# A four-layer transformer whose queues are ordered by a planner: the order by a hand-written key replaced by one that lays the steps out forwards and backwards, with durations from the trace

## The chip, the cores and the metric

The kernel runs on one core of a Trainium2 chip. Its time is in device microseconds (us): the time of one execution on the device, and over several runs their median. The engines are named as in the profile: PE is TensorE's matmuls and PEld its loads of weights, DVE is VectorE, ACT is ScalarE, POOL is GpSimd, SP is SyncE (which here only issues DMA transfers).

## The reference, cut to what matters

An input `x` of 2048 tokens by 128 channels passes through four layers. Each adds an attention and then a feed-forward part to `x`, and each part reads `x` after a norm over the channels without weights.

```python
x = x + attention_0(norm(x))  # 16 heads of 64, all 2048 keys, biases on q, k, v, out
x = x + experts(norm(x))      # 8 experts, each token to its argmax, at most 256 tokens each
x = x + attention_1(norm(x))  # 16 heads of 64, causal
x = x + mix(norm(x))          # sigmoid(xr Wr) * (relu(xk Wk)^2 Wv), xr and xk mixed with the token before
x = x + attention_2(norm(x))  # metric attention, 16 heads of 8
x = x + ffn_2(norm(x))        # relu, weights rounded to -1, 0, 1
x = x + attention_3(norm(x))  # 16 heads of 64, region mask, a bias from gelu/sigmoid features
x = x + ffn_3(norm(x))        # exact gelu, weights sign(w) * mean|w| by row
```

Within the experts a token's place is the count of earlier tokens with the same expert, so each chunk of tokens needs the counts of the chunks before it. All data are float32.

## The kernel before, in words

**Tiling.** `x` stays in SBUF as 16 tiles of 128 tokens. The three big attentions go through 8 pairs of heads, and each pair through 8 groups of 256 queries. A group is worked in this way: `score` (line 505) lets PE multiply keys and queries into PSUM banks; `scan` (L515) has DVE copy a bank to SBUF and take its minimum (queries carry the opposite sign, so the minimum is the peak); `spread_lowest` gathers the minima over partitions (POOL L561, DVE L564, and L569 on POOL where the layer has a bias) and hands them out (L575, on ACT, in the causal layer on POOL); `exps` (L587) has ACT take the exponentials and their sums; `turn` has DVE transpose blocks of 32 by 32 (L614), and in the layers without a causal mask PE transposes the last 128 keys of the group's last quarter instead (L622), which ACT copies back (L625); `weigh` (L646) multiplies by the values; `sum_up` (L667 on PE, L687 and L690) gives the inverse sums; `project_out` multiplies by the output weights (L704 on PE), divides on ACT (L714), and adds to `x` on POOL (L732). Projections of keys and queries are L399, of values L420. The pairs overlap: the next pair's projections and scores run beside the weighing of the last group.

**Between the attentions.** Here the work goes by chunks of tokens as soon as the last pair has left them. `normalise` takes statistics on DVE (L250), raises to a power on POOL (L255 to L257), scales (L260 on ACT; L265 on another engine for some tiles), transposes on PE (L271), and copies on ACT (L286). `experts` takes logits on PE (L886), subtracts the peak (L890, DVE), takes the exponential (ACT), chooses on DVE (`choose`, L894 to L901), counts on PE (`count`, L905), forms weights on DVE (`weights`, L910 to L916), transposes them on PE (`turn`, L920), multiplies by the biases (L924) and the experts (L947). After layer 1 follow the mix (`rest`: L1119 and L1142, L1123, gate L1127), the product that stands for layer 2's attention (L1131; its weights collapse to one 128 by 128 matrix, made ahead in `folded`), the ternary feed-forward (`feed_forward`: L989, activation L998, L1014), another norm, and the features of layer 3 (L1229, gelu L1234, L1242, sigmoid L1259, L1248). Weights of the last feed-forward part are binarised by `binary` (DVE L1283 to L1291, transposed on PE, L1301) while layer 3's attention runs.

**Steps, rings and the planner.** No instruction is issued where it is written down. Each piece of work is a `Step` with an engine, a believed duration in us, the steps that it follows, the buffers that it takes or uses, and a key: a tick of a time-table written by hand (`planner(tick, place)`), a place within the tick, and a running number. Buffers come from a `Ring` of a fixed number of tiles. In most rings the order in which steps take buffers is fixed by their keys; in three (PSUM tiles `MISC`, the norms' `MEANS` and `NORMED`) it is open. A step that takes a buffer waits for all users of the one it replaces.

At the end `run` (L120) puts all steps into the five engines' queues. It simulates the queues with the believed durations, 0.15 us for a hand-over between engines (`HOP`) and 1.3 us where ACT must load another function table. Each time it looks on each engine through the open steps in order of their key, takes the first that can start at once, or one that would be done before a better one starts, and of the five engines' finds the one that starts earliest; that step is issued next on its engine. Every engine then works through its queue in order, waiting by semaphores.

```python
for s in [next_[e]] if next_[e] else sorted(open_[e], key=lambda s: s.key):
    t = None if s.left else s.ready()
    if t is None:
        continue
    t = max(t, free[e])
    if found is None or t + us(s) <= found[0] + 0.1:
        found = (t, s)
    if found[0] <= free[e]:
        break
```

## Time and profile before

| what | value |
|---|---|
| median of 3 runs | 3465.9 us (3461.34 to 3470.4) |
| profiled execution | 3463.54 us |
| its span, first to last instruction | 3461.8 us |
| mean granted clock of TensorE | 0.987 of full speed |
| busy time of PE, DVE, ACT, POOL | 3378.0, 3211.7, 2810.9, 951.3 us |
| layer 0's attention, one pair in steady state | 147.1 us |
| layer 1's, one pair in steady state | 96.4 us |
| layer 3's, one pair in steady state | 149.5 us |
| loads of function tables on ACT | 30, 1283 ns each |

The profile is of one execution on the core. Its busy times are sums over the instructions of an engine; PE and PEld overlap each other. The stages follow one another in this order: a start of 27 us, layer 0's attention to about 1140 us, the experts and the start of layer 1 to about 1380, layer 1's attention to about 1990, mix, layer 2 and the start of layer 3 to about 2260, layer 3's attention to about 3340, and the end. The granted clock is what the throttle allows TensorE, as a share of full speed; a window of the trace gives its mean in that window. In a line on waits, the first name is the instruction that waits, and the one behind the arrow is what ended the wait. In a line of the timeline the bracket at the end holds the idle time ahead of an instruction, and what released it.

### The profile page before, as it was taken

How to read it: one execution, taken by the hardware profiler on the slowest of the kernel's cores; microseconds unless marked ns; L12 is line 12 of the kernel's file. 1: busy time of each engine (PE TensorE's matmuls, PEld its weight loads, DVE VectorE, ACT ScalarE, POOL GpSimd, SP SyncE). 2: the span in 40 equal slices, each digit the busy share in tenths (PEclk: the TensorE clock that was granted, in tenths of full speed). 3: DMA queues.
4: the chain of work that ended last, by engine and by line, in shares of the span. 5: the costliest groups of instructions: out<-in, count | busy, mean ns of one | idle time of the engine just before them, and what ended most of it. 6: DMA issues, size and time to landing. Idle time of an engine off the chain costs nothing.

```text
span 3461.8 us, 115408 instructions
## 1 busy us (share of the span) xinstructions
PE 3378.0 (98%) x46922; PEld 1819.8 (53%) x46922; DVE 3211.7 (93%) x8019; ACT 2810.9 (81%) x8712; POOL 951.3 (27%) x2821
## 2 busy tenths in 40 slices
PE   8999999999999899999999998899999999999999
PEld 3545454554545455555555654455555555555555
DVE  7999999999999878999999885699999999999996
ACT  5888888888888767888888876688888878888886
POOL 2121222212222343223232354222222222222233
PEclk9999999999999999999999999899999999999999
DMA  1000000000000000000000000000000000000000
GB/s 48 2 5 2 5 5 2 5 2 5 2 5 5 2 5 8 6 6 6 6 6 3 7 5 4 4 5 5 2 5 2 5 5 2 5 2 2 2 5 11
DMA packets 22960, 18.98 MB, mean 5 GB/s; under 512 B 3556, under 2 KB 21612, under 8 KB 22426
## 3 DMA queue, kind: packets, MB, share of 16 engines
q1 hardware_dynamic: 22362, 11.55, 1.2%
q8 instruction: 367, 6.01, 0.7%
q14 instruction: 167, 1.37, 0.1%
q0 software_dynamic: 64, 0.06, 0.0%
HBM read 10.60 MB, written 1.05 MB: 3 GB/s over the span
## 4 chain that ended last, share of the span: by engine, by line
PE 82%; DVE 11%; ACT 4%; issue 2%; POOL 1%; DMA 0%; SPq 0%; POOLq 0%; DVEq 0%; ACTq 0%
PE s L505 33%; PE o L646 32%; DVE e L515 5%; PE pp L399 5%; DVE e L614 3%; PE y L704 3%; PE pv L420 3%; ACT e L587 2%; PE t L622 2%; PE ps L667 1%; PE pe L947 1%; PE ph L989 1%; PE po L1014 1%; PE pt L271 0%; DVE st L250 0%
## 5 line engine op out<-in xcount | busy, mean ns | idle before, releaser
L587 ACT ACTIVATE e<-e,shift 128x512 f32<-128x512 f32 (+14 forms) x3072 | 1973.7, 649 | 26.3 <-POOL shift L575 18.6
L515 DVE TENSOR_SCALAR_CACHE_REDUCE e<-s 128x512 f32<-128x512 f32 (+15 forms) x3072 | 1659.0, 589 | 95.8 <-PE s L505 94.2
L505 PE MATMUL s<-kT,qT 64*32 64x512 f32 (+8 forms) x24576 | 1463.3, 535 | 20.6 <-DVE e L515 20.5
L614 DVE STREAM_TRANSPOSE e<-e 128x2048 f32<-128x2048 f32 (+10 forms) x768 | 1435.4, 1871 | 15.0 <-ACT e L587 12.9
L646 PE MATMUL o<-e,v 128*64 128x256 f32 (+1 forms) x10496 | 1272.6, 374 | 2.6 <-DVE e L614 2.4
L646 PEld LDWEIGHTS o<-e,v 128*64 128x64 f32 x10496 | 747.1, 137 | 549.3 <-issue 300.9
L505 PEld LDWEIGHTS s<-kT,qT 64*32 64x32 f32 x24576 | 417.0, 105 | 518.2 <-issue 220.6
L587 ACT ACTIVATION_READ_ACCUMULATOR e<-e,shift 128x1 f32 x3072 | 591.9, 193 | 0.0
L561 POOL COPY low<-low 32x8 f32<-32x8 f32 x1152 | 208.9, 181 | 1236.9 <-DVE e L515 1200.1
L732 POOL TENSOR_TENSOR x<-x,part 128x256 f32<-128x256 f32 x384 | 280.9, 731 | 269.3 <-ACT part L714 253.8
L575 ACT COPY shift<-shift 32x8 f32<-32x8 f32 x768 | 150.0, 195 | 134.7 <-POOL shift L569 88.1
L714 ACT ACTIVATE part<-y,r 128x128 f32<-128x128 f32 x768 | 217.6, 366 | 38.7 <-PE y L704 36.9
L515 DVE DVE_READ_ACCUMULATOR e<-s 128x1 f32 x3072 | 231.0, 75 | 0.0
L687 POOL TENSOR_TENSOR r<-r,inverse 128x4 f32<-128x4 f32 x128 | 130.3, 1018 | 322.5 <-ACT r L690 322.2
L399 PE MATMUL pp<-xT,w 128*128 128x512 f32 x384 | 213.7, 646 | 0.7 <-ACT xT L286 0.7
L646 PE MATMUL o<-e,va 128*64 128x128 f32 x1024 | 196.2, 273 | 0.0
L719 ACT COPY oT<-o 128x256 f32<-128x256 f32 x192 | 70.5, 367 | 154.6 <-PE o L646 153.9
L505 PE MATMUL s<-beyond,eye 64*32 64x32 bf16 x2560 | 160.0, 177 | 0.0
L704 PE MATMUL y<-w,oT 64*128 64x128 f32 x1536 | 139.0, 297 | 0.9 <-DVE bias L1255 0.4
L704 PEld LDWEIGHTS y<-w,oT 64*128 64x128 f32 x1536 | 101.6, 186 | 67.1 <-issue 23.6
L505 PEld LDWEIGHTS <-regions 64*32 64x32 bf16 x1024 | 66.3, 93 | 117.3 <-issue 84.1
L646 PEld LDWEIGHTS o<-e,va 128*64 128x64 f32 x1024 | 126.6, 138 | 0.0
(190 smaller groups left out, 2051.2 us busy)
## 6 DMA issues: line engine op xcount, KB each, us to landing
w<-in_L_wq SPq DMA_DIRECT2D x24, 64.0 KB, 1.9
w<-in_L_wk SPq DMA_DIRECT2D x24, 64.0 KB, 2.1
w<-in_L_wv SPq DMA_DIRECT2D x24, 64.0 KB, 2.1
w<-in_L_wo SPq DMA_DIRECT2D x24, 64.0 KB, 2.0
x<-in_x SPq DMA_DIRECT2D x4, 256.0 KB, 4.7
out_x<-x SPq DMA_DIRECT2D x3, 256.0 KB, 2.3
wo<-in_L_wo SPq DMA_DIRECT2D x1, 512.0 KB
moe_w<-in_moe_w SPq DMA_DIRECT2D x1, 512.0 KB
```

The lines of the kernel that those rows point to most:

```text
L399: nc.tensor.matmul(pp.t, lhsT=self.w.t[:, which, :], rhs=xT[:, cols(4 * c, 4)], start=True, stop=True)
L505: nc.tensor.matmul(s[h].t[on, bass.ds(first, size)], lhsT=lhsT, rhs=rhs, start=m == 0, stop=m == len(terms) - 1,)
L515: nc.vector.tensor_scalar(self.e(h)[:, i, 0:n], s.t[:, 0:n], 1.0, None, ALU.mult, ALU.min, accum_out=self.lows[j].t[:, 0, 4 * h + i % 4 : ...
L561: nc.gpsimd.tensor_copy(low.t[0:Q, c], low.t[bass.ts(c, Q), 0])
L575: (nc.gpsimd.tensor_copy if causal else nc.scalar.copy)(shift.t[bass.ts(c, Q)], first())
L587: nc.scalar.activation(e, e, AF.Exp, bias=self.shifts[j].t[:, 4 * h + i % 4 : 4 * h + i % 4 + 1], scale=-1.0, accum_out=self.sums.t[:, h, ...
L614: nc.vector.transpose(rows()[:, :, 0:n], rows()[:, :, 0:n])
L646: nc.tensor.matmul(self.o.t[bass.ds(DH * h, DH), i0:i1, :], lhsT=lhsT, rhs=self.e(h)[:, i0:i1, bass.ts(t, Q)], start=t == 0, stop=t == las ...
L687: nc.gpsimd.tensor_tensor(some, some, inverse, ALU.pow)
L704: nc.tensor.matmul(y[h].t[:, bass.ts(j, P)], lhsT=oT.t[half, bass.ts(j, P)], rhs=pair.w.t[half, 3, :], start=True, stop=True,)
L714: nc.scalar.mul(part.t[:, j, :], y[h].t[:, bass.ts(j, P)], r.t[:, j, h : h + 1])
L732: POOL, 0.74, lambda part=part: nc.gpsimd.tensor_tensor(xs, xs, part.t, ALU.add), [divided], uses=[part]
```

## The change

Two things change. First, `run` no longer takes the plan that comes from the keys. The old loop becomes `forward(rank, last)`, which sorts the open steps by a given rank; only with `last` does it issue anything. `backward()` takes the plan of the last `forward` and lays every step out again from the end: each as late as the steps behind it allow, in a gap of its engine that still holds it. Behind a step stand those that use its result, the step glued to it, and those that take its buffer over in the plan. The latest start is the step's new rank. `run` makes a plan by key, then three times a backward and a forward pass, and issues the one of these three plans that ends first in the planner's own times. The order within the rings is by key as before.

Second, about 35 believed durations are set to those of the trace. No instruction of arithmetic or transfer is added or removed. The built program loads ACT's function tables 25 times and not 30, and has 754 semaphore instructions and not 709 on POOL (ACT 535 and not 539, DVE 415 and not 408, PE 154 and not 152).

```diff
-        for _ in range(len(steps)):
-            best = None
...
+        def forward(rank, last):
+
+            for ring in rings:
+                ring.held = []
+            for s in steps:
+                s.left, s.since, s.end = len(s.after) + len(s.order) + (s in glued), 0.0, None
...
+                    for s in [next_[e]] if next_[e] else sorted(open_[e], key=lambda s: rank[s]):
...
+                s.begun, s.end = start, start + us(s)
...
+                for h in s.takes:
+                    if last:
+                        h.t = h.ring.make(h.called)
+                    h.ring.held.append(h)
+                if last:
+                    s.do()
...
+        def backward():
+
+            later = {s: list(h for h, data in heirs[s] if data) for s in steps}
+            for s in steps:
+                if s.then:
+                    later[s].append(s.then)
+            for ring in rings:
+                for h, g in zip(ring.held, ring.held[ring.bufs :]):
+                    for u in h.users:
+                        later[u].append(g.by)
+            end = max(s.end for s in steps)
+            busy, latest = [[(end + 1.0, end + 1e6)] for _ in range(5)], {}
+            for s in sorted(steps, key=lambda s: (-s.end, -s.begun)):
+                t = end
+                for b in later[s]:
+                    if b is not s:
+                        t = min(t, latest[b] - (HOP if b.engine != s.engine else 0.0))
+                gaps, us = busy[s.engine], s.end - s.begun
+                k = 0
+                while True:
+                    low = gaps[k + 1][1] if k + 1 < len(gaps) else -1e6
+                    top = min(t, gaps[k][0])
+                    if top - us >= low - 1e-6:
                         break
+                    k += 1
+                latest[s] = top - us
+                gaps.insert(k + 1, (top - us, top))
+            return latest
+
+
+        forward({s: s.key for s in steps}, False)
+        found = []
+        for _ in range(3):
+            rank = backward()
+            if not forward(rank, False):
+                break
+            found.append((max(s.end for s in steps), len(found), rank))
+        forward(min(found)[2], True)
```

```diff
-        t = add(PE, 0.2 * n, turn, scales, takes=[pt], uses=[xn])
+        t = add(PE, 0.04 + 0.115 * n, turn, scales, takes=[pt], uses=[xn])
...
-            us = max(0.2, 0.06 + 0.00168 * n) + (0.1 if causal else 0.07 if masked else 0.0)
+            us = max(0.15, 0.02 + 0.00168 * n)
+            more = 0.29 if causal else 0.27 if masked else 0.13
...
-            turned = [add(DVE, 0.06 + 0.00436 * n, do, made, uses=self.rows)]
+            turned = [add(DVE, 0.05 + 0.00426 * n, do, made, uses=self.rows)]
...
-                add(PE, 0.75, turn_apart, made, takes=[pt], uses=self.rows)
-                turned.append(add(ACT, 0.6, copy, uses=[pt] + self.rows))
+                add(PE, 0.55, turn_apart, made, takes=[pt], uses=self.rows)
+                turned.append(add(ACT, 0.47, copy, uses=[pt] + self.rows))
...
-        made = add(DVE, 1.3, choose, [made], uses=[r])
+        made = add(DVE, 1.7, choose, [made], uses=[r])
         add(PE, 0.4, count, [made] + masks, takes=[pc], uses=[r])
-        made = add(DVE, 1.2, weights, routed[-1:], uses=[r, pc])
+        made = add(DVE, 1.65, weights, routed[-1:], uses=[r, pc])
...
-        add(PE, 0.8, biases, [made], takes=[pb], uses=[pickT])
+        add(PE, 1.35, biases, [made], takes=[pb], uses=[pickT])
...
-            read.append(add(PE, 1.25, make, [made], takes=pe + [parts], uses=[moe_w]))
+            read.append(add(PE, 1.92, make, [made], takes=pe + [parts], uses=[moe_w]))
...
-                s = add(DVE, 0.2 + 0.002 * n, magnitude, last, takes=[] if last else [low], uses=[w] + ([low] if last else []))
-                last = [add(DVE, 0.2 + 0.0035 * n, signed, [s], uses=[w, low])]
+                s = add(DVE, 0.38 + 0.00168 * n, magnitude, last, takes=[] if last else [low], uses=[w] + ([low] if last else []))
+                last = [add(DVE, 0.5 + 0.0032 * n, signed, [s], uses=[w, low])]
```

The other durations change in the same manner, most of them by 0.02 to 0.7 us, among them the value projection's copy, the sums' copy, the products and the features.

## The prediction

> **What bounds the kernel now.** I read the page's busy times first, then its chain that ended last.

> ```profile
> PE 3378.0 (98%) x46922; PEld 1819.8 (53%) x46922; DVE 3211.7 (93%) x8019; ACT 2810.9 (81%) x8712; POOL 951.3 (27%) x2821
> PE 82%; DVE 11%; ACT 4%; issue 2%; POOL 1%; DMA 0%; SPq 0%; POOLq 0%; DVEq 0%; ACTq 0%
> ```

> TensorE is busy for 3378.0 of 3461.8 us, so 83.8 us is all its idle time. The change alters no instruction of arithmetic; it can win back idle time, the time lost to a lowered clock, and time that ACT or DVE put on the chain. To see where those lie I cut the run into stages with the table of windows (columns: window in us, its length, busy time of PE, PEld, DVE, ACT and POOL with their counts, granted clock, DMA share, GB/s). These are the two joints between layers, one pair of heads in layer 3's steady state, and a later pair in which weights are binarised:

> ```profile
> 1140.00:1380.00 240.00, 221.77 (x2851) 119.82 (x2854) 203.52 (x665) 164.96 (x557) 95.76 (x230) 0.94 0.02 5
> 1990.00:2260.00 270.00, 236.41 (x2391) 131.56 (x2390) 188.36 (x579) 195.83 (x502) 102.97 (x234) 0.92 0.02 5
> 2506.00:2655.50 149.50, 149.50 (x2009) 79.25 (x2009) 146.83 (x305) 124.64 (x373) 38.14 (x120) 1.00 0.01 4
> 2803.80:2961.80 158.00, 155.63 (x2050) 81.91 (x2049) 156.02 (x325) 127.82 (x382) 38.60 (x122) 0.99 0.01 4
> ```

> The steady state has no idle TensorE at all. The joints idle for 240 - 221.8 = 18.2 and 270 - 236.4 = 33.6 us, and their clock of 0.94 and 0.92 costs another 0.06 x 240 = 14 and 0.08 x 270 = 22 us. Three quarters of the reachable time is here. TensorE's waits name its releasers (engine, line, releaser: us in total, times, longest):

> ```profile
> PE pt L271 <- ACT xn L260: 26.5, 8, 12.4
> PE s L505 <- DVE e L515: 20.5, 28, 2.8
> PE pick_turned L920 <- DVE routes L916: 6.4, 3, 2.8
> PE pc L905 <- DVE routes L901: 5.2, 4, 1.9
> ```

> The transposes of a norm (L271) wait for its scaling; 12.4 of their 26.5 us is the start of the program. The routing of layer 0's experts (L905, L920) waits for VectorE; the scores wait for scans to free their banks.

> **The change, part by part.** The built orders of the two kernels hold the same arithmetic on each engine. ACT loads a function table 25 times, not 30, and POOL has 754 semaphore instructions, not 709. POOL is 27% busy and SyncE's queue holds the same loads in almost the same order (a weight lands 2 us after its issue), so I price both at nothing; if a weight came late, it would cost those 2 us once.

> *Routing of the experts.* TensorE's timeline shows the wait in chunk 0, and what came after it:

> ```profile
> 1147.50 0.38 PE L905 MATMUL pc<-routes,earlier 128*128 128x32 f32 x2 [0.73 <-DVE routes L901]
> 1148.03 0.71 PE L704 MATMUL y<-w,oT 64*128 64x128 f32 x8
> 1151.53 1.01 PE L920 MATMUL pick_turned<-ident,routes 128*8 128x128 f32 x4 [2.79 <-DVE routes L916]
> 1153.21 2.07 PE L924 MATMUL pb<-moe_b,pickT 8*128 8x128 f32 x8 [0.66 <-ACT pickT L937]
> ```

> The planner believed 1.3 and 1.2 us for `choose` and `weights` and now believes 1.7 and 1.65, so it puts more TensorE work between them. By the new order, chunk 0 has four weighings and a query projection's part (0.8 us) ahead of L905: 0.73 goes, while the 2.79 stays. Chunk 1 has a projection and four weighings (1.0 + 1.05) between L905 and L920: its 2.79 becomes about 1.4 and its 0.72 nearly 0. Chunk 2 puts two projections ahead of L905, not one: 1.83 becomes 0.8. Chunk 3 puts 1.7 us ahead: 1.87 becomes 0.17, and 0.81 becomes 0.6. That is 0.73 + 1.39 + 0.65 + 1.03 + 1.70 + 0.21 = 5.7. What is taken from later work leaves a shorter queue there, so I take -4.5, bounds 0 and -5.7.

> *Clock.* After that stall the biases (L924) took 2.07 us; in chunk 2 the same row took 1.15. The windows 1153 to 1157 and 1213 to 1219 have a granted clock of 0.50 and 0.60, each after a stall of 2.79. A dip costs about 2 to 3 us (6 us at 0.60 loses 2.4). One of the two 2.79s shrinks, and the two of 1.8 go: I take one dip, -3. Bounds: 0, and -20 if about half of the 36 us of clock in both joints comes back. [...]

> *Layer 1 to layer 3.* The last four tiles pass norm, mix, product, FFN and norm one after another while little else is left:

> ```profile
> 2117.26 0.66 PE L271 MATMUL pt<-ident,xn 128*128 128x128 f32 x4 [1.86 <-ACT part L714]
> 2127.57 5.19 PE L646 MATMUL o<-e,v 128*64 128x256 f32 x48
> 2143.86 1.54 PE L271 MATMUL pt<-ident,xn 128*128 128x128 f32 x6 [6.74 <-ACT xn L260]
> ```

> In the new order the 48 weighings of 5.19 us and a product of 0.71 come ahead of the transposes at 2117.26. Of these 5.9 us, 1.86 falls in the stall there, so the norm may start 4.0 later; but the chain's later steps are then free of the 5.19. Between +4.0 and -1.2 I take +1, near the lower end, since TensorE idles 6.74 soon after. Moved out of the way: the mix of chunk 2 (L1142) no longer stands behind a weighing that took 0.61 + 3.50 and takes 1.95 at full clock elsewhere (-1.8, the part that is no stall and no longer slow); a first norm on POOL between another's powers and its scaling (-1.3, one such L255 to L257); a projection (L399, 1.13) now ahead of the features' weighing (-1). Before this, from 2010 to 2117, TensorE idles 107 - 97.6 = 9.4 us at clock 0.95; some steps there are reordered, none clearly for the better: -1. Together -4. Bounds: +5.9 with all of the weighing on the path, and -15 with the 9.4 and the 5.4 of its clock gone.

> *Function tables.* On ACT's timeline a load takes 1.28 us, and the exponential after it starts 1.30 after it:

> ```profile
> 2211.10 1.28 ACT L587 ACT_TABLE_LOAD   x1
> 2212.40 0.72 ACT L587 ACTIVATE e<-e,shift 128x512 f32<-128x512 f32 x1
> ```

> Three of the five saved loads are in layer 1's end, two in the last FFN, where ACT is on the chain: 2 x 1.28 = 2.6, and one of the three, 1.3, since the joint's waits are on ACT for half of their time: -3.9, bounds 0 and -6.4. [...]

> *Binarised weights.* Seven DVE pieces lay in one lump of 8.2 us (2798.6 to 2806.9), and TensorE ran dry behind the scans:

> ```profile
> 2804.00:2808.00 4.00, 1.78 (x16) 1.24 (x18) 3.86 (x9) 1.42 (x3) 0.00 (x0) 1.00 0.01 2
> 2808.00:2812.00 4.00, 4.00 (x40) 1.26 (x34) 4.00 (x9) 2.21 (x7) 0.39 (x2) 0.57 0.00 0
> ```

> The pair took 158.0 and the one ahead of it 148.4, against 149.5: 8.5 - 1.1 = 7.4 lost. The new order spreads the pieces one to a gap (DVE has 149.5 - 146.8 = 2.7 of slack in a pair) but for the last three, 0.93 + 1.25 + 2.1 = 4.3 in a row. With the loss in proportion, 7.4 x 4.3 / 8.2 = 3.9 stays: -3.5, bounds 0 and -5.5.

> *Start.* One more projection stands ahead of the first scores (1 us at a cold clock), and one less after them: +0.5, bounds -0.5 and +1.5.

> *Steady state.* Rings of buffers are still handed out by the hand-written key, so scans, weighings and scores keep their sequence, and DVE's order in a pair of layer 0 is identical. What moves is the transpose of a group's last quarter (L622), now ahead of about 5 us of TensorE work that it followed. I price it at 0 and cover it under the rivals.

> Sum: -4.5 - 3 - 4 - 3.9 - 3.5 + 0.5 = -18.4, from the profiled execution of 3463.5 (span 3461.8 and 1.7 around it): 3445.1. The median shown is 2.4 above the profiled time, so the forecast is 3447.5, told as 3448.

> **The rivals.**

> *Out of step, slower.* L622 waits for the last exponentials of its quarter, on an ACT that is 124.6 of 149.5 us busy, and TensorE works in order: whenever ACT is late, scores and weighings behind it stand. Now the weight loads of L622 wait on ACT's exponentials 24 times in 128, 6.8 us in all, about 0.28 each: the cover is the work ahead of it, and the change takes it away. At 0.14 us a group, 128 groups of layers 0 and 3 lose 17.9, the whole gain; from 0.14 + 10.4 / 128 = 0.22 on it is slower by over 0.3%. If each group waits the 0.28, it loses 35.8 less the gain of 18.4 at most, +17; I take 0.23 or +12: 3478. Against it: VectorE bounds layer 0 as closely as TensorE, so half of such waits may be free.

> *Gains eaten at the joints.* Stalls that go from one place return at the next, since the chain of chunks there is ACT, POOL and DVE work of unchanged length; only the tail's tables (-2.6), half of the binarising (-1.8) and half of the routing (-2.3) stay: -7, or 3459.

> *It does not do what it says.* The order by key seeds the search but is not among the three candidates, and ring order by key binds every plan; if lateness matters little, the plan is merely another, and the time 3466. I count it with the case above.

> *The clock comes back.* If most stalls fall below what lowers the clock, -20 takes the place of -3: about -36, or 3430.

> **How the numbers follow.** Forecast 0.45, the clock 0.12, gains eaten or nothing done 0.23, out of step 0.20. About 0.3%, or 10.4 us, is what a measurement of this kernel can tell from no change. The forecast and the clock case are below 3455.5: faster 0.57; same 0.23; slower 0.20. The range runs from 3428, within 2 us of the clock case, to 3474, which takes in the milder part of the slower case and leaves its far part out; the forecast's own range by its bounds is 3435 to 3457.

> **What would show it.** Right: L920's waits fall from 6.4 to about 4.8 and L905's from 5.2 to under 1.5; 25 table loads; the pair with the binarising takes some 154; the pairs at 147.1 and 149.5 stay; the joints shrink by some 6 each. Wrong: pairs in layers 0 or 3 over 0.5 us longer, with L622 waiting on L587; or L271's wait for xn grown at the second joint by more than 4; or a lower clock in either joint.

## The result, and the profile after

The changed kernel takes 3458.8 us (3456.6 to 3461.8, 14 runs), the kernel before 3469.8 beside it (3461.3 to 3472.7, 14 runs): a ratio of 0.9973, interval 0.9965 to 0.9981. A second comparison gave 0.9972 (0.9963 to 0.9982). The forecast was 3448, a ratio of 0.9948 to the median shown. Direction and range were right. The forecast gain, 0.52%, is about double the measured 0.27%; between the two profiled executions, for which the sum was made, it is four times what came: the profiled one took 3458.9 (span 3457.2), 4.6 us less than that of before, for 18.4. Of the 8 to 11 us between the medians, the rest is in executions of the kernel before that no profile shows: its two profiled ones took 3463.5 and 3464.1, 9 of its 14 in the first comparison 3468 to 3473.

Busy times and chain on the page of after:

```profile
PE 3371.3 (98%) x46922; PEld 1808.7 (52%) x46922; DVE 3216.3 (93%) x8019; ACT 2801.9 (81%) x8707; POOL 950.9 (28%) x2821
PE 83%; DVE 12%; ACT 3%; issue 2%; POOL 0%; DMA 0%; SPq 0%; DVEq 0%; POOLq 0%; ACTq 0%
```

TensorE still bounds it. The windows of after (columns as before): the two joints, a pair in layer 3, and the pair with the binarising.

```profile
1140.00:1380.00 240.00, 221.55 (x2860) 119.22 (x2856) 209.58 (x679) 170.12 (x572) 96.48 (x234) 0.95 0.02 5
1990.00:2260.00 270.00, 230.03 (x2252) 130.80 (x2239) 183.80 (x560) 185.68 (x471) 99.08 (x225) 0.90 0.02 4
2563.80:2713.30 149.50, 149.50 (x2010) 79.28 (x2008) 148.13 (x311) 123.87 (x374) 38.30 (x120) 1.00 0.01 4
2713.40:2865.50 152.10, 151.97 (x2018) 80.47 (x2018) 151.21 (x314) 124.69 (x375) 38.18 (x120) 1.00 0.01 4
```

The second joint idles more (40.0 us of 270, 33.6 before) at a lower clock (0.90, 0.92). The pair with the binarising is nearly full. TensorE's waits in after:

```profile
PE pt L322 <- ACT xn L311: 29.7, 8, 12.4
...
PE o L698 <- DVE e L666: 6.4, 4, 3.7
PE pick_turned L972 <- DVE routes L968: 4.2, 2, 3.0
```

The routing's waits shrank, as forecast; the norms' grew, and weighings now wait longer for transposes (L698 for L666: 6.4 us, in before 2.4).

To place the difference I cut each run at the starts of the output products (L704 before, L756 after; the timeline shows each group's eight matmuls). They come in the same order in every kernel here, 0 to 191. Stretches in us:

| run | to 8 | 8-56 layer 0 | 56-64 experts | 64-72 start of layer 1 | 72-120 layer 1 | 120-128 way to layer 3 | 128-152 | 152-160 binarising | 160-end | span |
|---|---|---|---|---|---|---|---|---|---|---|
| before | 233.2 | 878.8 | 179.4 | 149.1 | 555.1 | 266.6 | 448.2 | 156.7 | 594.8 | 3461.8 |
| after | 232.4 | 884.8 | 170.9 | 157.4 | 545.9 | 274.7 | 447.2 | 152.1 | 591.7 | 3457.2 |
| e2 durations alone | 237.4 | 884.5 | 171.1 | 159.3 | 546.0 | 282.5 | 447.8 | 153.4 | 593.8 | 3475.8 |
| e3 ranks alone | 231.3 | 878.9 | 175.5 | 146.8 | 552.1 | 266.4 | 448.7 | 155.3 | 592.9 | 3447.9 |
| e4 attention's | 230.5 | 884.7 | 174.0 | 154.3 | 545.8 | 268.1 | 447.2 | 152.3 | 591.6 | 3448.4 |
| e7 old norms, features | 227.9 | 884.7 | 174.3 | 148.3 | 545.8 | 266.7 | 447.2 | 152.1 | 593.2 | 3440.0 |
| e8 causal's | 230.0 | 878.9 | 177.9 | 164.8 | 545.8 | 264.1 | 448.7 | 154.7 | 593.2 | 3458.1 |
| e10 causal's, routing's | 233.3 | 878.9 | 173.7 | 151.3 | 546.3 | 260.6 | 447.5 | 155.0 | 594.1 | 3440.7 |
| e11 old norms | 231.6 | 883.6 | 174.4 | 147.1 | 545.9 | 271.2 | 447.2 | 152.2 | 591.7 | 3444.9 |
| e12 old features | 232.4 | 884.7 | 170.6 | 157.1 | 545.9 | 274.1 | 447.2 | 152.1 | 591.7 | 3455.9 |

From before to after: -0.8, +6.0, -8.5, +8.3, -9.2, +8.1, -1.0, -4.6, -3.1, in sum about -4.6. So the change gained 27 us and lost 22. Each stretch is read from one profile, and product 64 lies within a joint: the experts and the start of layer 1 together took 328.5 us before and 328.3 after. Three places were not in my sum or had the wrong sign.

**The start of layer 1 (+8.3).** PE's timeline of after:

```profile
1376.85 0.62 PE L698 MATMUL o<-e,v 128*64 128x256 f32 x2 [1.09 <-DVE e L666]
1381.14 7.34 PE L698 MATMUL o<-e,v 128*64 128x256 f32 x46 [3.67 <-DVE e L666]
```

48 weighings stand in TensorE's queue ahead of the projections that the next pair's scores need. They wait for a transpose that ends at 1381.1, and run at half clock up to 1385.1 (from start to start 11.6 us; 48 took 5.2 in before). The next pair's first scores come at 1394.0; in before at 1382.8, where no such block stands. But the block alone does not make the stretch longer. It stands with the same waits in e4, e7, e9, e10 and e11 below, where the stretch is 147.1 to 154.3. This is e11, with 147.1:

```profile
1372.84 7.05 PE L698 MATMUL o<-e,v 128*64 128x256 f32 x46 [3.67 <-DVE e L666]
```

From product 64 to the block there are 88.8 us in after, 79.0 in e7 and e11, 84.5 in e9 (154.2 in all). So what sets after apart from these runs arose ahead of the block. About 4 us of it are the lowered clock, as e9 shows (below); the rest isn't placed. Before has dips of the clock here too (5.1 us lost to them in this stretch, 8.5 in after), so how the +8.3 itself divides stays open.

**Layer 1's pairs (-1.45 each).** PE's timeline around one score step of width 320, in before:

```profile
1659.66 0.79 PE L505 MATMUL s<-kT,qT 64*32 64x320 f32 x16
...
1661.52 0.89 PE L505 MATMUL s<-kT,qT 64*32 64x320 f32 x12 [0.29 <-DVE e L515]
...
1663.44 1.13 PE L399 MATMUL pp<-xT,w 128*128 128x512 f32 x2
```

And in after:

```profile
1660.81 0.79 PE L556 MATMUL s<-kT,qT 64*32 64x320 f32 x16
...
1662.32 1.12 PE L450 MATMUL pp<-xT,w 128*128 128x512 f32 x2
1663.38 1.00 PE L556 MATMUL s<-kT,qT 64*32 64x320 f32 x18
```

In before two halves follow each other, and the second waits bit by bit for banks that the scans free: 3.79 us. In after a projection stands between, and the halves take 1.51 + 1.43. The same happens at width 160 (0.68). The list of waits hardly shows it (0.5 us a pair), since it is spread in pieces too short to be listed.

**The way to layer 3 (+8.1).** PE's timeline of after:

```profile
2115.96 1.95 PE L698 MATMUL o<-e,v 128*64 128x256 f32 x16
2117.84 0.66 PE L322 MATMUL pt<-ident,xn 128*128 128x128 f32 x4
2118.42 1.73 PE L698 MATMUL o<-e,v 128*64 128x256 f32 x16
...
2132.91 1.54 PE L322 MATMUL pt<-ident,xn 128*128 128x128 f32 x6 [6.67 <-ACT xn L311]
...
2142.68 1.50 PE L322 MATMUL pt<-ident,xn 128*128 128x128 f32 x4 [5.47 <-ACT xn L311]
```

The norm with which the last chunks' chain begins (2117.84) comes 126.4 us after product 120, in before 121.7. 48 weighings that followed it in before precede it now. So less is left to fill the next wait, the 6.67 (none stood there in before), and the chain from that norm to the first scores of layer 3 takes 86.6 us for 83.7.

### The profile page after: what moved, and what is told of

Read it like the earlier page. It is cut to its first block, busy times and chain, and to the rows that moved or that the text cites. A ratio compares the mean times of both kernels' runs of the same rounds, so it can differ in the third digit from the quotient of the medians.

```text
span 3457.2 us, 115453 instructions
## 1 busy us (share of the span) xinstructions
PE 3371.3 (98%) x46922; PEld 1808.7 (52%) x46922; DVE 3216.3 (93%) x8019; ACT 2801.9 (81%) x8707; POOL 950.9 (28%) x2821
## 3 DMA queue, kind: packets, MB, share of 16 engines
HBM read 10.60 MB, written 1.05 MB: 3 GB/s over the span
## 4 chain that ended last, share of the span: by engine, by line
PE 83%; DVE 12%; ACT 3%; issue 2%; POOL 0%; DMA 0%; SPq 0%; DVEq 0%; POOLq 0%; ACTq 0%
PE s L556 33%; PE o L698 32%; DVE e L566 6%; PE pp L450 5%; DVE e L666 4%; PE y L756 3%; PE pv L471 3%; PE t L674 2%; ACT e L639 1%; PE ps L719 1%; PE pe L999 1%; PE ph L1041 1%; PE po L1066 1%; PE pt L322 0%; DVE st L301 0%
## 5 line engine op out<-in xcount | busy, mean ns | idle before, releaser
L639 ACT ACTIVATE e<-e,shift 128x512 f32<-128x512 f32 (+15 forms) x3072 | 1972.7, 648 | 23.7 <-POOL shift L627 16.4
L556 PE MATMUL s<-kT,qT 64*32 64x512 f32 (+8 forms) x24576 | 1448.9, 533 | 17.7 <-DVE e L566 16.4
L666 DVE STREAM_TRANSPOSE e<-e 128x2048 f32<-128x2048 f32 (+10 forms) x768 | 1436.8, 1873 | 18.8 <-ACT e L639 18.0
L698 PE MATMUL o<-e,v 128*64 128x256 f32 (+1 forms) x10496 | 1275.4, 374 | 6.6 <-DVE e L666 6.4
L698 PEld LDWEIGHTS o<-e,v 128*64 128x64 f32 x10496 | 738.4, 137 | 565.5 <-issue 309.3
L698 PE MATMUL o<-e,va 128*64 128x128 f32 x1024 | 196.4, 274 | 0.0
L771 ACT COPY oT<-o 128x256 f32<-128x256 f32 x192 | 71.0, 370 | 125.1 <-PE o L698 124.6
L756 PE MATMUL y<-w,oT 64*128 64x128 f32 x1536 | 137.9, 297 | 1.0 <-ACT oT L771 0.7
L756 PEld LDWEIGHTS y<-w,oT 64*128 64x128 f32 x1536 | 100.9, 186 | 57.5 <-issue 46.5
L698 PEld LDWEIGHTS o<-e,va 128*64 128x64 f32 x1024 | 126.8, 138 | 0.0
```

What stands on the lines that cost most here:

```text
L556: nc.tensor.matmul(s[h].t[on, bass.ds(first, size)], lhsT=lhsT, rhs=rhs, start=m == 0, stop=m == len(terms) - 1,)
L639: nc.scalar.activation(e, e, AF.Exp, bias=self.shifts[j].t[:, 4 * h + i % 4 : 4 * h + i % 4 + 1], scale=-1.0, accum_out=self.sums.t[:, h, ...
L666: nc.vector.transpose(rows()[:, :, 0:n], rows()[:, :, 0:n])
L698: nc.tensor.matmul(self.o.t[bass.ds(DH * h, DH), i0:i1, :], lhsT=lhsT, rhs=self.e(h)[:, i0:i1, bass.ts(t, Q)], start=t == 0, stop=t == las ...
L756: nc.tensor.matmul(y[h].t[:, bass.ts(j, P)], lhsT=oT.t[half, bass.ts(j, P)], rhs=pair.w.t[half, 3, :], start=True, stop=True,)
```

## The experiments

**e1, the kernel before once more.**

> The kernel before, unchanged, for a second profile and for how far its own executions spread (3461 to 3473 us so far, against 3456.6 to 3461.8 after). Theory that the spread is the clock: a profile near 3470 shows 5 us or more of additional time at the lowered clock, with pairs of 147.1, 96.4 and 149.5 us unchanged. Rival, that the spread is the steady state falling into another step: the pairs of layer 0 are 147.7 or more in a profile near 3470, and the lowered clock is as long as before. Ratio to the kernel before: 1.000 within 0.001.

Ratio 1.0003 (0.9994 to 1.0012). Its profile (span 3462.3) has the stretches of before within 0.8 us, with pairs of 147.1, 96.4 and 149.5. A profile near 3470 did not come, so neither theory was tried by one. The record lists the mean granted clock of 87 executions of the kernel before: the 23 of 3468 us or more had 0.984 to 0.986, the 64 shorter ones 0.986 to 0.989. That agrees with the first theory, the clock; where in the run it fell, and whether the pairs kept their length, stays open.

**e2, the new durations without ranks.**

```diff
-        forward(min(found)[2], True)
+        forward({s: s.key for s in steps}, True)
```

> The new durations with the order by key, no ranks. Theory A (the durations order the steady states and make both lengthened joints; the ranks win the rest): layer 1's pairs at 95.0, layer 0's at 147.7, the stretch between the 64th and the 72nd output product 155 us or more (149.1 before, 157.4 after), that between the 120th and the 128th 272 or more (266.6 before, 274.7 after); in sum 3462 to 3472 us, no faster than before. Rival B (the durations bring the gain, the ranks nothing): 3452 to 3460.

3478.1 us, ratio 1.0041 (1.0028 to 1.0054): the durations alone make the kernel slower. They bring layer 1's -9.1 and the binarising's, layer 0's +6, and both bad joints, worse than in after (159.3, 282.5). Theory A holds in its places; its time came 6 us above its range. Rival B falls.

**e3, the ranks with the old durations.** The diff's second part is left out, the first kept.

> The old durations with the forward and backward passes. Theory A: layer 0's pairs stay at 147.1, the stretch from the 64th to the 72nd output product stays near 149, that from the 120th to the 128th near 266; layer 1's pairs 95.6 to 96.4; the tail shorter by 2 to 3 us; 3448 to 3456 us, faster than after. Rival B: 3462 to 3470, no faster than before.

3451.1, ratio 0.9968 (0.9956 to 0.9979), span 3447.9: the ranks alone are worth 13.9 us of span, durations alone cost 14.0, both together gain 4.6. Layer 0 stays, neither joint has grown. ACT loads its tables 30 times here and 25 times in e2, so the loads went with the durations; yet the end (160 on) is shorter here by 1.9 and in e2 by 1.0. Layer 1's pairs come down to 95.95 by the ranks alone. The time lost to the lowered clock is 35.8 us here, 43.4 in before, 54.7 in e2.

**e4, the new durations in the attention's steps alone,** with ranks.

> Forward and backward passes, the new durations only in the attention's own steps (projections, scores, scans, transposes, weighing, sums, output); norms, experts, features, weights and the mix keep the old ones. Theory A: layer 1's pairs at 95.0 and layer 0's at 147.7 come from these durations; if the long stretches at 64 to 72 and 120 to 128 come from the others, both are back near 149 and 266 and the time is 3442 to 3450; if they come from these, the time stays at 3455 to 3462. Rival B: as after, 3457 to 3461.

3450.9, ratio 0.9965 (0.9952 to 0.9977), span 3448.4. Both steady states and the binarising's gain come from the attention's durations. The way to layer 3 is 268.1, near its old length; the start of layer 1 lies in between (154.3), and the time came just above the range of that case, 3442 to 3450.

**e5, the changed kernel again.**

> The changed kernel as it is, to be compared with the others on one chip. If its gain of 0.27% was partly the kernel before running at 3470 us in that comparison, the ratio here is 0.998 to 0.999 (3458 to 3464 us); if not, 0.997 again.

Ratio 0.9972 (0.9963 to 0.9982), as in the first comparison, and the changed kernel at 3457.9. But that does not decide the question: 11 of the 23 executions of the kernel before took 3468 us or more here too. To the median of the other 12, 3463.1, the ratio is 0.9985, within what was expected if the long executions made part of the gain. So about half of the measured gain lies in the long executions of the kernel before.

**e7, e11, e12: the old durations for norms and features.**

```diff
-        made = [add(DVE, 0.6, lambda: stats(0), after, takes=[mv])]
+        made = [add(DVE, 0.57, lambda: stats(0), after, takes=[mv])]
...
-        t = add(PE, 0.04 + 0.115 * n, turn, scales, takes=[pt], uses=[xn])
+        t = add(PE, 0.2 * n, turn, scales, takes=[pt], uses=[xn])
...
-            add(PE, 0.9, make, L3.ready[c], takes=[ph, hm[j]])
+            add(PE, 1.0, make, L3.ready[c], takes=[ph, hm[j]])
```

e7 has both, e11 the norms' two edits, e12 the features' three.

> The changed kernel, with the old durations for the norms' statistics and transposes and for the features of layer 3 alone. Theory A (these durations pull the last weighings of layer 1 ahead of the norm that the chain to layer 3 begins with): the stretch from the 120th to the 128th output product is 265 to 269 again, the weighings stand behind that norm, layer 1's pairs stay at 95.0; 3448 to 3453 us. Rival E (the ranks or the attention's durations lengthen it): 273 or more, 3456 to 3461.

> The changed kernel with the old durations for the norms' statistics and transposes alone. If the norms' durations make the stall at the start of layer 1 (64th to 72nd output product 157), it is 148 to 150 here; if they also pull the weighings ahead at the way into layer 3 (274.7), that is 266 to 269, else 272 or more. Planned by the kernel itself: 148.4 and 271.6. 3444 to 3455 us.

> The changed kernel with the old durations for the features of layer 3 alone. Planned by the kernel itself: 152.4 from the 64th to the 72nd output product and 269.8 from the 120th to the 128th. If the features' durations make the long way into layer 3, that is 266 to 269 here with the stall at the start of layer 1 still there (157); 3449 to 3453 us. If not: 273 or more, 3456 to 3460.

e7: 3443.5, ratio 0.9935 (0.9920 to 0.9949). e11: 3446.8, 0.9945 (0.9926 to 0.9963). e12: 3457.4, 0.9973 (0.9964 to 0.9982), as after. e7 came 4.5 us below theory A's range, since the start of layer 1 fell too. Taken back in the changed kernel, the norms' durations shorten the start of layer 1 by 10.3 us (147.1) and lengthen the stretch ahead of it by 3.5; they are no cause by themselves, for e4, e8 and e10 have the old ones too, and 151.3 to 164.8 there. On the way to layer 3 they give 3.5 of the 8 us; the rest falls only if both go back. PE's timeline in e7 shows the norm ahead of 48 weighings again:

```profile
2100.52 0.66 PE L322 MATMUL pt<-ident,xn 128*128 128x128 f32 x4
...
2102.26 1.95 PE L698 MATMUL o<-e,v 128*64 128x256 f32 x16
...
2107.84 1.95 PE L698 MATMUL o<-e,v 128*64 128x256 f32 x16
...
2110.08 1.74 PE L698 MATMUL o<-e,v 128*64 128x256 f32 x16
```

The norm (2100.52) comes 119.7 after product 120. Over the ten runs of the table, the way to layer 3 goes with the number of layer 1's last weighings that are left behind this norm: 48 or 64 left, 260.6 to 268.1 us (before, e3, e4, e7, e8, e10); 32 left, 271.2 (e11); 16 left, 274.1 to 282.5 (after, e12, e2).

**e8 and e10: new durations in the causal layer's attention,** old ones in the other attentions; e10 has the new ones of experts, weights and binarising as well.

```diff
-            us = max(0.15, 0.02 + 0.00168 * n)
-            more = 0.29 if causal else 0.27 if masked else 0.13
+            us = max(0.15, 0.02 + 0.00168 * n) if causal else 0.06 + 0.00168 * n + (0.07 if masked else 0.0)
+            more = 0.29 if causal else 0.0
```

> Forward and backward passes, the new durations for the attention's steps in the causal layer only, the old ones everywhere else. Theory A (each layer's steady state follows its own durations): layer 0's pairs 147.1, layer 1's 95.0, the stretch from the 120th to the 128th output product 264 to 268, but that from the 64th to the 72nd lengthened to 152 or more; 3445 to 3451 us. If the old durations of the experts spare the stretch from 64 to 72 as well (147), 3439 to 3445.

> Forward and backward passes, old durations for the norms and features and for the attention outside the causal layer, new ones for the rest. If the parts add up (theory A), layer 0's pairs are 147.1 and the rest as in the run with the old norms and features: 3436 to 3441 us. Rival F (the joints are a throw of the dice for every set of durations): pairs of 147.1 and 95.0 as well, but the stretches from 56 to 72 or from 120 to 128 off by over 6 us; 3445 to 3460.

e8: 3454.8, ratio 0.9970 (0.9959 to 0.9981); e10: 3442.0, 0.9927 (0.9914 to 0.9940), with e7 the fastest run here. A pair of layer 0 in e10:

```profile
527.00:674.10 147.10, 147.10 (x1876) 73.97 (x1874) 146.38 (x305) 124.49 (x373) 32.00 (x88) 1.00 0.02 4
```

So each steady state follows its own layer's durations: 147.1 with the old, 147.7 with the new in layer 0, 95.0 with the new in layer 1. The joints don't add up: the start of layer 1 is 164.8 in e8 and 151.3 in e10, the way to layer 3 264.1 and 260.6. e8's profile is of one of its longer executions (3459.8; the median is 3454.8), with 15.4 us lost to the clock at the start of layer 1 alone, for 8.5 in after, so 164.8 is probably more than usual. e8's median came 4 us above theory A's range, e10 1 us above. Rival F is right on the joints, not on the time.

**e6, e9, e13, e14: filling TensorE's waits,** to learn whether the lowered clock is on the path. All are the changed kernel with useless transposes of the identity in one or two places; e6 and e9 put them ahead of a waiting transpose, e13 and e14 behind the work before the wait. The edit of e13:

```diff
             nc.tensor.matmul(pc.t[:, n : 2 * n], lhsT=ones, rhs=flat(MASK), start=True, stop=True)
+            for i in range(18 if t0 == 0 else 0):
+                nc.tensor.transpose(pc.t[:, bass.ts(1 + i % 3, P)], ident, ident)
```

> The changed kernel, with useless transposes of the identity (32 and 24) put on TensorE ahead of those of two norms, where it waits 6.67 us at 2132.9 and 5.47 us at 2142.7; the real transposes overwrite them. The order is unchanged. Theory C (a window of the clock with little TensorE work halves the clock in the next, and the slow work after it is on the path): the 20.5 us at half clock from 2129 shrink to under 10, and the stretch from the 120th to the 128th output product from 274.7 to 265 to 270; 3449 to 3454 us. Rival D (the chain of norms on ACT, POOL and DVE sets that stretch, and the clock does not matter): it stays within 1.5 us of 274.7, or grows by what the transposes overrun; 3457 to 3461.

> The changed kernel, with useless transposes of the identity ahead of the transposes of the routing weights: 18 in chunk 0, where TensorE waits 2.96 us at 1154.3 and the granted clock is 0.50 from 1153.0 to 1163.2, and 8 in chunk 1, where it waits 1.26; the real transposes overwrite them. At 0.116 us each they fit into the waits, and the order is unchanged. Theory C (the clock follows how much of a window of 3.4 us TensorE worked): the dip at 1153 goes, the biases behind it take 1.05 and not 2.0 us, the first two experts' products 1.9 and not 3.7; the stretch up to the 64th output product is 3 to 5 us shorter; 3453 to 3456 us. Rival D (the routing chain on DVE, ACT and POOL sets the stretch): the dip may go, but the 64th output product moves by less than 1 us; 3457 to 3459.

e6: 3462.4, ratio 0.9990 (0.9981 to 0.9999). e9: 3455.8, 0.9969 (0.9958 to 0.9981). Neither filled the wait that it was meant to fill. In e9 the filling itself waited 2.02 us for its bank, which the counts' reader still held, then ran 4.07 us at half clock; in e6 it came behind the 6.67 us wait, where another chunk's transposes wait first, and delayed the chain: the way to layer 3 grew to 278.1. What e6 does show is that 4.9 us put on TensorE at that place cost 3.4.

e9 shows something else, by chance. But for the filling, TensorE's order is that of after; its work came to lie otherwise against the steps in which the clock changes (last section), and two dips of after (10.2 us near 1307, 3.4 near 1214) are missing. Near 1307 TensorE waits 1.24 us in both; the clock behind this wait is 0.50 in after and 1.00 in e9. The first experts' products of that chunk, in after, then in e9:

```profile
1311.45 3.78 PE L999 MATMUL pe<-moe_w,xT 128*128 128x512 f32 x4
```

```profile
1310.85 1.98 PE L1001 MATMUL pe<-moe_w,xT 128*128 128x512 f32 x4
```

Product 67 comes 53.4 us after product 64 in e9, 57.7 in after (57.5 in e5): without this dip, which loses 5.1 us at half clock, the work is 4.1 to 4.3 us earlier, and some 3 of them are left at product 72. From product 60 to 61, where the other dip is missing, e9 takes 33.6 for 34.8. So the lowered clock is on the path in these two places. It isn't everywhere: before has a dip near 1180 that e1 lacks, and from product 58 to 60 they take 58.7 and 58.9.

> The changed kernel, with 18 useless transposes of the identity behind the counts of chunk 0, in columns of the counts' own bank that nothing reads, so that they need to wait for nothing and fill 2.1 us of the wait of 2.96 ahead of the routing weights' transposes. Theory C (too little work in a window of 3.4 us halves the clock of the next): the dip of 10.2 us at 1153.0 goes, the biases take 1.05 and not 2.07, the first experts' products 1.9 and not 3.8; the 64th output product comes 2 to 5 us earlier; 3453 to 3456 us. Rival D (the chain on DVE, ACT and POOL sets this stretch): the dip goes, the product moves by under 1 us; 3457 to 3459.

> The changed kernel, with 44 useless transposes of the identity (5.1 us) behind the last transposes that TensorE does before it waits 6.67 us on the way into layer 3, in columns of that bank that nothing reads. Theory C: the 20.5 us at half clock from 2129.2 shrink to 13.7 or less, the product behind the wait takes 1.1 and not 2.1, and the stretch from the 120th to the 128th output product shrinks by 2 to 5 us; 3452 to 3456 us. Rival D: the dip shrinks, that stretch stays within 1 us of 274.6; 3457 to 3459.

e13: 3458.3, ratio 0.9980 (0.9971 to 0.9989). PE's timeline shows the filling and the waits behind it:

```profile
1148.84 2.16 PE L960 MATMUL pc<-ident 128*128 128x128 f32 x18
...
1152.62 0.60 PE L974 MATMUL pick_turned<-ident,routes 128*8 128x128 f32 x4 [0.98 <-DVE routes L970]
1154.71 2.07 PE L978 MATMUL pb<-moe_b,pickT 8*128 8x128 f32 x8 [1.49 <-ACT pickT L991]
```

The wait shrank from 2.96 to 0.98, but the dip only began one step of the clock later and lasted 6.8 us, not 10.2. The biases still ran at half clock (2.07) and now waited 1.49 for ACT, and the stretch to product 64 is 170.9, as in after. e14: 3458.9, 0.9982 (0.9973 to 0.9990): the dip shrank from 20.5 to 17.1 us, and the way to layer 3 took 275.6. Here the filling stood on the chain itself, for ACT's copy of the bank waited for it (5.92 us, in after 1.12), and the wait behind it was still 6.41 us. So shortening these two dips by 3.4 us did not shorten either stretch, but neither run took a dip away. What all the dips together cost stays open.

## Why the prediction was right or wrong

- **Routing (-4.5).** Right in place: -8.5 to product 64, of which the time lost to the clock is 3.4 (from 10.2 to 6.8). L920's waits went from 6.4 to 4.2 (4.8 forecast), and those of L905 for VectorE (5.2) are no longer listed.
- **"What is taken from later work leaves a shorter queue there."** I turned this sentence into a discount of 1.2 us and set no term for the start of layer 1; that was the first step that failed. The next stretch lost 8.3, all of the gain. That is the rival "gains eaten at the joints" (0.23, 3459), which came nearest in time too, though not by its sum: the joints took more than the joints' gains, and layer 1's pairs paid for it. The 48 weighings at its end are no sufficient cause, for e11 has them in 147.1 us; one dip of the clock in chunk 3's routing is worth about 4 us (e9); what else lengthened this stretch stays open.
- **Layer 1 to layer 3 (-4): the step that failed by most, 12 us.** I had found the 48 weighings pulled ahead of the norm, set the bounds +4.0 and -1.2, and took +1 "near the lower end, since TensorE idles 6.74 soon after". The norm came 4.7 later, and the idle time of 6.74 became two waits of 6.67 and 5.47, for the weighings had been what filled the first of them. The three steps "moved out of the way" did not shorten the chain, which took 86.6 us for 83.7. Measured +8.1, beyond my upper bound of +5.9; the time lost to the lowered clock there also rose, from 22.2 to 27.3 us (half of the time at half clock), where my clock term had only gains.
- **Steady state (0).** Wrong twice, and by luck nearly cancelling: layer 0 +6.0, layer 1 -9.2. I had not compared layer 1's order step by step. The slower rival's mechanism did not come: the weight loads of L622's transposes waited for exponentials 4 times, 2.0 us, instead of 24 times, 6.8. Layer 0's +6.0 is 0.65 us in each of five pairs, and 2.7 in the last (product 48 to 56). In a pair, DVE is busy 146.6 us for 146.4 and waits 1.0 for 0.7 for scores; the rest isn't placed.
- **Binarised weights (-3.5):** -4.6, and the lump is broken up as forecast; e4 and e10 show that the new durations of the attention do this, not those of the binarising. **Tables (-3.9):** the end became 3.1 shorter, but e3 with 30 loads and e2 with 25 show that the count alone does not explain it. **Start (+0.5):** -0.8; a projection's two products take 2.07 us at 14.37 in after, but the one that was added stands in a block of four at 21.47 that takes 2.02.
- **Clock (-3):** wrong; the time lost to it rose from 43.4 to 49.6 us over the run, though by e9 some of that time does cost. I had gone by the length of single stalls, 2.79 and 1.8 us; in the traces a step ahead of a dip had no wait over 0.48 us and one that kept the clock had 1.44 (last section).

By subtraction alone, without the joints' +16.4 and layer 0's +6.0 the span would have been 3434.8; no run had that. The fastest two, e7 and e10, reach 3440.0 and 3440.7.

## What to carry to other kernels

When a planner's durations or ranks change, judge steady states and joints apart: here the steady states followed the durations of their own layer in all runs, within 0.5 us, while the joints jumped by 3 to 16 us with small edits elsewhere, partly by where the waits fell against the clock's steps (without one dip of 10.2 us the work came 4.1 to 4.3 us earlier in e9). Test the parts alone, since ranks (-14 us) and durations (+14) had opposite signs. Where filling work lies beside a serial chain, ask whether it is left behind the chain's first step: moved ahead, 48 weighings delayed the chain by 4.7 us here, and its next wait was 6.67 us.

## What the runs showed of the hardware that was not expected

```profile
1303.20:1306.60 3.40, 1.68 (x33) 1.11 (x33) 3.09 (x18) 3.40 (x16) 1.45 (x2) 1.00 0.00 0
1306.60:1310.00 3.40, 2.92 (x31) 1.58 (x32) 2.74 (x12) 1.94 (x7) 0.72 (x4) 0.50 0.00 0
```

```profile
1150.75:1154.15 3.40, 1.49 (x15) 0.82 (x13) 2.91 (x12) 2.48 (x9) 1.45 (x2) 1.00 0.00 0
1154.20:1157.60 3.40, 2.89 (x9) 2.28 (x10) 1.50 (x6) 1.88 (x6) 0.54 (x3) 0.50 0.01 2
```

```profile
1302.10:1305.50 3.40, 2.63 (x58) 2.06 (x42) 3.16 (x15) 3.40 (x17) 0.41 (x1) 1.00 0.00 0
1305.50:1308.90 3.40, 2.16 (x44) 1.16 (x43) 3.09 (x15) 3.06 (x13) 1.59 (x5) 1.00 0.00 0
```

A step with 1.68 of 3.40 us busy (e13: 1.49) is followed by one at 0.50, and no single wait in e13's was longer than 1.49. In e9 the waits of after's step fell into two, busy for 2.63 and 2.16 us, and the clock stayed. So in these rows the clock went with the work in a step, and not with the longest wait: one step ahead of a dip had no single wait over 0.48 us (before, near 3426), while one that kept the clock had 1.44 (after, near 2081) and one 1.58 (e2). In before, after, e2, e3 and e4 nearly all steps ahead of a dip were busy for under 0.7 of their time, and steps that kept the clock for 0.53 or more; the two ranges overlap. A few dips followed busier steps (0.76 in e2, 0.87 in e4), among them one at 163.03 us in before, behind 3.40 of 3.40 us busy; these are unexplained.
